# A four-layer graph network on one Trainium2 core: a column load moved to another queue, source tiles weighted on another engine, weights folded at another place

## The chip, the cores and the metric

The kernel runs on one core of a Trainium2 chip. A core has five engines that run at the same time, each with its own instruction stream, in order: TensorE (PE, matmuls), VectorE (DVE), ScalarE (ACT), GpSimd (POOL) and SyncE (SP, which here only starts DMAs). A DMA can be started from SP, ACT or POOL, and it stands in that engine's stream like any other instruction. Work areas are SBUF (125 or 128 partitions are used here) and PSUM, where matmuls accumulate. The metric is the device time of one execution in microseconds (us).

## The reference

A graph with N = 3125 nodes, 50,000 edges and D = 256 features goes through four layers. Each layer is x + gnn(norm(x)) + mix(norm(x)), then x + ffn(norm(x)). Layers 1, 2 and 3 have graph attention in the gnn part. Cut to what matters:

```python
h = (x @ W.T).reshape(n, heads, out_ch)
alpha_src = jnp.sum(h * a_src, axis=-1)
alpha_dst = jnp.sum(h * a_dst, axis=-1)
e = jax.nn.leaky_relu(alpha_src[src] + alpha_dst[dst], NEG_SLOPE)
m = jax.ops.segment_max(e, dst, num_segments=n)
e = jnp.exp(e - m[dst])
s = jax.ops.segment_sum(e, dst, num_segments=n)
alpha = e / (s[dst] + 1e-16)
out = jax.ops.segment_sum(alpha[:, :, None] * h[src], dst, num_segments=n)
```

In layers 1 and 2 this runs twice: first with four heads (of 128 features in layer 1, 64 in layer 2), then, after the bias b1, an elu and a product with W2, with one head of 256. In layer 3 it runs once, with four heads of 64; a bias gat_b is added, and the result is added to the layer's input copy before an elu. The ffn of layer 1 is a mixture of experts with a shared dense part: every node goes through the shared part, and each node's two best private experts get a copy of its row.

## The kernel before

Nodes are cut into NT = 25 tiles of P = 125. The adjacency is kept as a dense 3125 x 3125 matrix of edge counts in DRAM (`adj`).

**Edge sums.** `gat_products` does the attention for all edges by matmuls. An edge's exponential is split into factors of the source and of the target, so that exp(leaky_relu(..)) becomes max(target row, source factor) times a source weight `gpre` (L1180). First, all 25 source tiles of h, with one column of ones per head, are multiplied by `gpre` in place (L1187 to L1189): every third tile on GpSimd, the others on VectorE. Then the target tiles are taken in groups of five (875 or 750 target columns at a time in `sums_by_feature`, which is used for heads of 64). For each group the target factors are spread over all partitions (`spread`, a matmul with the identity at L189, evicted by VectorE at L78 or ScalarE at L80 into `rows`). Within a group the loop goes over the 25 source tiles s: a piece `a` of the adjacency is loaded by SP, VectorE makes t = max(rows, over) * a for each head (L1232, or L1308), and TensorE adds t and h of the tile into the accumulators `acc` (L1237, or L1313 and L1322). `gat_products` is called five times: layer 1 heads, layer 1 last, layer 2 heads, layer 2 last, layer 3.

**Last weights.** `gat_heads` loads W2 into the tile `w2a` (L1402), its bias b1, and folds the vectors a_src2 and a_dst2 into two more columns of `w2a` (`folded`, L973 multiplies, L974 reduces). It is called after the layer's input is normed, projected and mixed. Then `gat_spans` (from L1128) and the edge sums follow.

**Layer 3's local branch.** `l3_local` adds gat_b to the whole tile `local` (125 x 6400) in one GpSimd addition (L2037), and each finished target tile to its part of `local` on VectorE (L2042). `local` is loaded from DRAM in front of it, by ScalarE's queue, in two parts of 112 and 13 partitions (`halves`, L886 and L887).

**Layer 1's columns.** In layer 1's ffn each node's row with four more numbers (D + 4 columns) is scattered by GpSimd into two rows of a buffer `f1_rows` in DRAM (L2272, 50 scatters of 125 rows). The four last columns of all 8000 rows are then loaded back into `ends` (125 x 64 x 4), again by `halves` on ScalarE's queue; VectorE makes indices of it (L1585 to L1594). The shared dense part follows in program text: hidden layers with a Gelu on ScalarE (L605), products `ps_out` on TensorE, additions to X on VectorE (L1604).

**The order.** The program is traced by a tile scheduler. It places the instructions of each engine in an order of its own, with semaphores where tiles depend on each other, and it moves instructions past others of the program text. Pools of tiles reuse memory: a load into a tile waits until whoever used the place before has finished. Within an engine the order is then fixed. In the built program the additions of layer 0's last X (L931) and the first norms XN (L153) of layer 1 follow each other on VectorE; in layer 2 the XN of the first tiles stand among the last additions of X (L1653).

Of the kernel before, what the change touches and what calls it, by code (L numbers as in the profile page):

```python
# [11 lines left out]
F32 = mybir.dt.float32  # L12
# [9 lines left out]
D = 256  # L22
E = 50000
P = 125
NT = N // P
# [35 lines left out]
class Net:  # L61
# [1106 lines left out]
    def gat_products(self, far, h, al, heads, width, loops, use):  # L1168
# [3 lines left out]
        with ExitStack() as es:  # L1172
# [14 lines left out]
            for s in range(NT):  # L1187
                eng = nc.gpsimd if s % 3 == 2 else nc.vector
                eng.tensor_mul(h[:, s], h[:, s], pre[:, s, :, None].to_broadcast([P, heads, width + 1]))  # L1189
            if width < 96:  # L1190
                self.sums_by_feature(es, mine, over, h, heads, width, loops, use)
                return
# [20 lines left out]
            for g in range(NG):  # L1213
# [10 lines left out]
                for s in range(NT):  # L1224
                    a = ap.tile([P, GW], F32, name="a")
                    self.load_edges(a, self.adj_rows(), s, g)
                    if loops and s // GB == g:
                        blk = a[:, (s % GB) * P:(s % GB + 1) * P]
                        nc.vector.tensor_add(blk, blk, self.ident[:P, :P])
                    t = tp.tile([P, heads, GW], F32, name="t")  # L1230
# [21 lines left out]
    def sums_by_feature(self, es, mine, over, h, heads, width, loops, use):  # L1252
# [35 lines left out]
        for i0, n in COLUMNS:  # L1288
# [10 lines left out]
            for s in range(NT):  # L1299
                a = ap.tile([P, most], F32, name="a")  # L1300
                self.halves(nc.sync, a[:, :w], self.adj_rows()[s * P:(s + 1) * P, i0 * P:i0 * P + w])
                if loops and i0 <= s < i0 + n:
                    blk = a[:, (s - i0) * P:(s - i0 + 1) * P]
                    nc.vector.tensor_add(blk, blk, self.ident[:P, :P])
                t = []
# [86 lines left out]
    def gat_heads(self, prefix, h, al, h2, al2, heads, width, loops, eps):  # L1392
# [4 lines left out]
        h2v = h2[:, :, 0, :D]  # L1397
        with ExitStack() as es:
            wp = es.enter_context(self.pool("tg_w"))
            kp = es.enter_context(self.pool("tg_k", 2))  # L1400
            w2 = wp.tile([128, chunks, D + 2], F32, name="w2a")
            nc.sync.dma_start(w2[:, :, :D], self.ins[prefix + "W2"].rearrange("(c p) m -> p c m", p=128))  # L1402
            b1 = self.rows(wp, prefix + "b1")
            with self.pool("tg_f") as fp:
                self.folded(fp, w2[:, :, :D], chunks, 1, [prefix + "a_src2", prefix + "a_dst2"],
                            w2[:, :, D:])
# [125 lines left out]
    def l1_ffn(self, given):  # L1532
# [8 lines left out]
        with ExitStack() as es:  # L1541
# [10 lines left out]
            with ExitStack() as es2:  # L1552
# [27 lines left out]
                self.halves(nc.scalar, ends, rows[:, D:].rearrange("(q p) c -> p q c", p=P))  # L1580
# [154 lines left out]
    def layer1(self):  # L1735
# [4 lines left out]
        with self.pool("g1_h2") as low:  # L1740
            last = self.last_terms(low)
            with self.pool("g1_h") as hp:
                with self.pool("in1") as ip:
# [3 lines left out]
                self.gat_heads(pre, h, al, *last, 4, 128, False, 1e-16)  # L1747
# [189 lines left out]
    def layer2(self):  # L1937
        pre = "L2_gnn_"
        with self.pool("g2_h2") as low:
            last = self.last_terms(low)  # L1940
            with self.pool("g2_h") as hp:
                with self.pool("in2") as ip:
# [3 lines left out]
                self.gat_heads(pre, h, al, *last, 4, 64, True, 0.0)  # L1946
# [766 lines left out]
```

## Time and profile before

| What | Value |
|---|---|
| Median of 3 runs | 6647.1 us (6640.66 to 6662.06) |
| Profiled execution, its own time | 6652.58 us |
| Its span in the trace | 6650.5 us |
| Granted TensorE clock, mean | 0.911 |
| Edge sums, layer 1: heads, last | 1655 to 2304 us, 2328 to 2680 us |
| Layer 1, scatters of rows, load of `ends` | 2695 to 2769 us, 2772 to 2779 us |
| Edge sums, layer 2: heads, last | 3628 to 4150 us, 4155 to 4460 us |
| Edge sums, layer 3 | 5510 to 6048 us |

The profile names an instruction by its engine, its source line (L189 is line 189 of the kernel before), its operation, the tile that it writes and those that it reads. In a row of the timeline the first number is the start in us from the begin of the span, the second the length of the row, at its end stands the number of instructions joined in it, and in brackets the idle time of that engine before it, with what ended the idle time. A name ending in q (ACTq, SPq) is the DMA-issuing part of that engine's stream.

### The profile page before, as it was taken

To read this page: it belongs to the slowest core of one execution; us is meant where nothing else is said; L and a number is where in the kernel's file an instruction comes from. 1 tells how busy PE (TensorE), PEld (TensorE's weight loads), DVE (VectorE), ACT (ScalarE), POOL (GpSimd) and SP (SyncE) were. 2 spreads that over 40 slices of the span, in tenths; PEclk is the share of its full clock that TensorE was granted. 3 is DMA by queue.
4 is the path that set the end of the run, shared out by engine and by line. 5 is a ranking of instruction groups with operands and counts; after the bars stand their busy time and mean duration, and the time that the engine had idled before them with its cause. 6 is when DMAs were issued, how large, how long until landed. Compare 5 with 4: busy or idle time off the path is not lost. (4 is left out here: it accounts for less than half of the span.)

```text
span 6650.5 us, 80016 instructions
## 1 busy us (share of the span) xinstructions
PE 5730.2 (86%) x30063; PEld 3902.5 (59%) x30063; DVE 3734.0 (56%) x7804; ACT 1695.3 (25%) x3532; POOL 917.8 (14%) x714
## 2 busy tenths in 40 slices
PE   5887999996999998699976999999878887997876
PEld 4555975664899877468853344776534443333644
DVE  7734333128877644115036887546378888886433
ACT  2433432331011100113333011002256560003411
POOL 0000100004000012301111000120334552002021
PEclk7888999997999999789987999999889998998888
DMA  2644668101222143215520222430332223222132
GB/s 80 106 64 67 181 197 244 31 5 68 62 63 63 45 140 111 66 51 168 173 88 20 83 81 61 138 112 1 88 46 57 57 50 94 71 77 69 46 120 94
DMA packets 436886, 571.69 MB, mean 86 GB/s; under 512 B 130447, under 2 KB 321372, under 8 KB 432687
## 3 DMA queue, kind: packets, MB, share of 16 engines
q1 hardware_dynamic: 363116, 468.81, 26.4%
q10 hardware_dynamic: 44907, 68.00, 3.7%
q0 software_dynamic: 28416, 29.15, 1.6%
q8 instruction: 252, 4.13, 0.3%
q14 instruction: 195, 1.59, 0.1%
HBM read 450.03 MB, written 115.55 MB: 85 GB/s over the span
## 5 line engine op out<-in xcount | busy, mean ns | idle before, releaser
L1232 DVE SCALAR_TENSOR_TENSOR t<-rows,over,a 125x625 f32<-125x625 f32 x750 | 619.6, 866 | 426.3 <-PE acc L1237 418.9
L1308 DVE SCALAR_TENSOR_TENSOR t<-rows,over,a 125x750 f32<-125x750 f32 (+1 forms) x800 | 793.3, 1045 | 75.4 <-PE acc L1322 70.6
L1313 PE MATMUL acc<-t,g_h 125*64 125x375 f32 (+1 forms) x3200 | 596.5, 500 | 12.2 <-DVE t L1308 12.2
L1237 PE MATMUL acc<-g_h,t 125*125 125x129 f32 x5000 | 574.5, 274 | 6.2 <-ACT x L1363 3.5
L1237 PE MATMUL acc<-h,t 125*125 125x257 f32 x2500 | 558.4, 383 | 19.8 <-DVE t L1232 10.0
L1237 PEld LDWEIGHTS acc<-g_h,t 125*125 125x125 f32 x5000 | 566.2, 188 | 10.8 <-ACT x L1363 4.2
L1237 PEld LDWEIGHTS acc<-h,t 125*125 125x125 f32 x2500 | 467.3, 189 | 103.9 <-PE acc L1237 18.8
L1313 PEld LDWEIGHTS acc<-t,g_h 125*64 125x64 f32 x3200 | 220.0, 136 | 340.1 <-issue 238.8
L1322 PE MATMUL acc<-t,g_h 125*32 125x375 f32 (+1 forms) x3200 | 359.1, 496 | 0.0
L2215 POOL TENSOR_TENSOR bx<-h,crow 128x500 f32<-128x500 f32 (+1 forms) x224 | 263.7, 1195 | 308.9 <-issue 79.3
L2221 PE MATMUL y<-bx,ident 128*128 128x500 f32 (+1 forms) x448 | 222.7, 611 | 66.0 <-POOL bx L2215 64.3
L931 DVE SCALAR_TENSOR_TENSOR X<-ps_out,prob,X 125x256 f32<-125x256 f32 x200 | 87.9, 479 | 338.7 <-PE ps_out L181 338.5
L2212 DVE TENSOR_TENSOR_SCAN h<-da,state,bx 128x500 f32<-128x500 f32 (+1 forms) x224 | 246.2, 1130 | 18.3 <-ACT da L2210 15.8
L605 ACT ACTIVATE h<-ps_hidden,L_ffn_b,bn_s 128x500 f32<-128x500 f32 (+1 forms) x224 | 160.4, 723 | 350.9 <-PE ps_hidden L181 330.1
L1322 PEld LDWEIGHTS acc<-t,g_h 125*32 125x32 f32 x3200 | 99.6, 109 | 236.3 <-issue 235.5
L181 PE MATMUL ps_hidden<-xbt,w 128*128 128x250 f32 x928 | 206.2, 380 | 22.3 <-ACT xbt L166 21.9
L864 PE MATMUL agg<-h,few 125*125 125x257 bf16 x1875 | 212.6, 274 | 4.3 <-ACT few L861 2.2
L864 PEld LDWEIGHTS <-few 125*125 125x125 bf16 x1875 | 207.9, 137 | 6.1 <-ACT few L861 3.3
L181 PE MATMUL ps_out<-w,hb 128*125 128x256 f32 x928 | 205.0, 379 | 0.0
L181 PEld LDWEIGHTS ps_hidden<-xbt,w 128*128 128x128 f32 x928 | 175.1, 191 | 49.0 <-ACT xbt L166 28.6
L181 PE MATMUL ps_hidden<-XNT,L_ffn_W 128*128 128x500 f32 (+1 forms) x448 | 195.8, 562 | 0.0
L181 PEld LDWEIGHTS ps_out<-w,hb 128*125 128x125 f32 x928 | 174.0, 188 | 25.9
(765 smaller groups left out, 9461.0 us busy)
## 6 DMA issues: line engine op xcount, KB each, us to landing
a<-adj SPq DMA_DIRECT2D x500, 273.4 KB
a<-adj SPq DMA_DIRECT2D x150, 328.1 KB
arow<-adj SPq DMA_DIRECT2D x25, 1367.2 KB
adj<-block SPq DMA_DIRECT2D x22, 1531.2 KB
w<-in_L_ffn_W1p SPq DMA_DIRECT2D x29, 1024.0 KB
w<-in_L_ffn_W2p SPq DMA_DIRECT2D x29, 1024.0 KB
crow<-crows ACTq DMA_DIRECT2D x96, 250.0 KB
a<-adj SPq DMA_DIRECT2D x50, 382.8 KB
```

What stands on the lines that cost most here:

```text
L181: self.nc.tensor.matmul(ps, lhsT[k], rhs[k], start=(k == 0), stop=(k == n - 1))
L605: self.nc.scalar.activation(out[:, f, :], ps[:, :nt], func, **kw)
L864: nc.tensor.matmul(acc[b][:P, :D + 1], few[:, b * P:(b + 1) * P], h[k][:, s, :], start=(s == 0 and k == 0), stop=(s == NT - 1 and k == 2))
L931: nc.vector.scalar_tensor_tensor(x, ps, prob[:, g + j, e:e + 1], x, op0=ALU.mult, op1=ALU.add)
L1232: nc.vector.scalar_tensor_tensor(t[:, hd, :], rows[:, hd, :], over[:, s, hd:hd + 1], a, op0=ALU.max, op1=ALU.mult)
L1237: nc.tensor.matmul(acc(b, hd), t[:, hd, b * P:(b + 1) * P], h[:, s, hd, :], start=(s == 0 and first), stop=(s == NT - 1), skip_group_check ...
L1308: nc.vector.scalar_tensor_tensor(t[hd][:, :w], rows[hd][:, :w], over[:, s, hd:hd + 1], a[:, :w], op0=ALU.max, op1=ALU.mult)
L1313: nc.tensor.matmul(acc[k][c][q * width:(q + 1) * width, :c1 - c0], h[:, s, 2 * k + q, :width], t[2 * k + q][:, c0:c1], start=(s == 0), sto ...
L1322: nc.tensor.matmul(acc[pairs][c][hd * 32:(hd + 1) * 32, :c1 - c0], h[:, s1, hd, width:].to_broadcast([P, 32]), t1[hd][:, c0:c1], start=(s1 ...
L2212: nc.vector.tensor_tensor_scan(h[:, :w], da[:, :w], bx[:, :w], state[:, c, s:s + 1], op0=ALU.mult, op1=ALU.add)
L2215: nc.gpsimd.tensor_mul(bx[:, :w], h[:, :w], crow[:, :w])
L2221: nc.tensor.matmul(acc[c][:, :w], self.ident, terms[c][:, :w], start=(s == 0), stop=(s == S - 1))
```

## The change

Four edits, independent of each other in the text:

1. The weighting of the source tiles leaves the head of `gat_products`. A function `weigh(s)` does it on ScalarE, one activation with a scale per head, and is called in the loop over source tiles while the first group is worked on. This applies to all five calls.
2. The load of W2 and b1 and the fold move from `gat_heads` into `last_weights`, which is called before `layer_input` in layers 1 and 2. Their tiles live in the pool of h instead of a pool of `gat_heads`.
3. In layer 3, `local` is loaded by GpSimd's queue, and gat_b is added per target tile by VectorE in `use`, to the finished sums, instead of to all of `local` by GpSimd.
4. In layer 1's ffn, `ends` is loaded by GpSimd's queue.

```diff
@@ -1184,11 +1184,13 @@
             nc.vector.tensor_tensor(mine, mine, far[:, None, heads:].to_broadcast([P, NT, heads]), op=ALU.min)
             nc.vector.tensor_add(mine, mine, most)
             nc.scalar.activation(mine, mine, AF.Exp, scale=-0.8)
-            for s in range(NT):
-                eng = nc.gpsimd if s % 3 == 2 else nc.vector
-                eng.tensor_mul(h[:, s], h[:, s], pre[:, s, :, None].to_broadcast([P, heads, width + 1]))
+
+            def weigh(s):
+
+                for hd in range(heads):
+                    nc.scalar.activation(h[:, s, hd, :], h[:, s, hd, :], AF.Copy, scale=pre[:, s, hd:hd + 1])
             if width < 96:
-                self.sums_by_feature(es, mine, over, h, heads, width, loops, use)
+                self.sums_by_feature(es, mine, over, h, weigh, heads, width, loops, use)
                 return
             lp = es.enter_context(self.pool("gq_p", 2))
             ap = es.enter_context(self.pool("gq_a", 4))
@@ -1227,6 +1229,8 @@
                     if loops and s // GB == g:
                         blk = a[:, (s % GB) * P:(s % GB + 1) * P]
                         nc.vector.tensor_add(blk, blk, self.ident[:P, :P])
+                    if g == 0:
+                        weigh(s)
                     t = tp.tile([P, heads, GW], F32, name="t")
                     for hd in range(heads):
                         nc.vector.scalar_tensor_tensor(t[:, hd, :], rows[:, hd, :], over[:, s, hd:hd + 1], a,
@@ -1249,7 +1253,7 @@
             while jobs:
                 advance()
 
-    def sums_by_feature(self, es, mine, over, h, heads, width, loops, use):
+    def sums_by_feature(self, es, mine, over, h, weigh, heads, width, loops, use):
 
 
 
@@ -1302,6 +1306,8 @@
                 if loops and i0 <= s < i0 + n:
                     blk = a[:, (s - i0) * P:(s - i0 + 1) * P]
                     nc.vector.tensor_add(blk, blk, self.ident[:P, :P])
+                if i0 == 0:
+                    weigh(s)
                 t = []
                 for hd in range(heads):
                     t.append(tp.tile([P, most], F32, name="t"))
@@ -1389,21 +1395,25 @@
         yield
         nc.vector.scalar_tensor_tensor(x, x, 0.0, m, op0=ALU.max, op1=ALU.add)
 
-    def gat_heads(self, prefix, h, al, h2, al2, heads, width, loops, eps):
+    def last_weights(self, pool, prefix, wide):
+
+        chunks = wide // 128
+        w2 = pool.tile([128, chunks, D + 2], F32, name="w2a")
+        self.nc.sync.dma_start(w2[:, :, :D], self.ins[prefix + "W2"].rearrange("(c p) m -> p c m", p=128))
+        b1 = self.rows(pool, prefix + "b1")
+        with self.pool("tg_f") as fp:
+            self.folded(fp, w2[:, :, :D], chunks, 1, [prefix + "a_src2", prefix + "a_dst2"], w2[:, :, D:])
+        return w2, b1
+
+    def gat_heads(self, weights, h, al, h2, al2, heads, width, loops, eps):
 
         nc = self.nc
         wide = heads * width
         chunks = wide // 128
         h2v = h2[:, :, 0, :D]
+        w2, b1 = weights
         with ExitStack() as es:
-            wp = es.enter_context(self.pool("tg_w"))
             kp = es.enter_context(self.pool("tg_k", 2))
-            w2 = wp.tile([128, chunks, D + 2], F32, name="w2a")
-            nc.sync.dma_start(w2[:, :, :D], self.ins[prefix + "W2"].rearrange("(c p) m -> p c m", p=128))
-            b1 = self.rows(wp, prefix + "b1")
-            with self.pool("tg_f") as fp:
-                self.folded(fp, w2[:, :, :D], chunks, 1, [prefix + "a_src2", prefix + "a_dst2"],
-                            w2[:, :, D:])
             nc.gpsimd.memset(h2[:, :, :, D:D + 1], 1.0)
 
             def use1(pp, i, acc, eps):
@@ -1577,7 +1587,7 @@
                             for i in range(NT) for k in range(2)], "all pairs' rows differ")
 
                 ends = ep.tile([P, 2 * MAXB, 4], F32, name="ends")
-                self.halves(nc.scalar, ends, rows[:, D:].rearrange("(q p) c -> p q c", p=P))
+                self.halves(nc.gpsimd, ends, rows[:, D:].rearrange("(q p) c -> p q c", p=P))
                 who, first, w0, w1_ = (ends[:, :, k].rearrange("p (b j) -> p b j", j=2) for k in range(4))
                 e = number[:, :, None].to_broadcast([P, MAXB, 2])
                 two = [t.rearrange("p (b j) -> p b j", j=2) for t in (part, own)]
@@ -1740,11 +1750,12 @@
         with self.pool("g1_h2") as low:
             last = self.last_terms(low)
             with self.pool("g1_h") as hp:
+                weights = self.last_weights(hp, pre, 512)
                 with self.pool("in1") as ip:
                     xn, xnt = self.layer_input(ip)
                     h, al = self.l1_mix(xn, xnt, lambda: self.gat_project(
                         hp, xnt, pre, "W1", 4, ("a_src1", "a_dst1"), "g1"))
-                self.gat_heads(pre, h, al, *last, 4, 128, False, 1e-16)
+                self.gat_heads(weights, h, al, *last, 4, 128, False, 1e-16)
             self.l1_ffn(lambda xn, xnt: self.gat_last(pre, *last, False, 1e-16, xn, xnt))
 
 
@@ -1939,11 +1950,12 @@
         with self.pool("g2_h2") as low:
             last = self.last_terms(low)
             with self.pool("g2_h") as hp:
+                weights = self.last_weights(hp, pre, 256)
                 with self.pool("in2") as ip:
                     xn, xnt = self.layer_input(ip)
                     h, al = self.l2_mix(xn, xnt, lambda: self.gat_project(
                         hp, xnt, pre, "W1", 4, ("a_src1", "a_dst1"), "g2"))
-                self.gat_heads(pre, h, al, *last, 4, 64, True, 0.0)
+                self.gat_heads(weights, h, al, *last, 4, 64, True, 0.0)
             self.l2_ffn(lambda xn, xnt: self.gat_last(pre, *last, True, 0.0, xn, xnt))
 
 
@@ -2034,11 +2046,10 @@
             nc.vector.tensor_scalar(less, less, LN_EPS16, 87.0, op0=ALU.add, op1=ALU.min)
             nc.scalar.activation(less, less, AF.Exp)
 
-            nc.gpsimd.tensor_add(out, out, gb[:, None, :].to_broadcast([P, NT, D]))
-
             def use(pp, i, acc, eps):
                 x = kp.tile([P, D], F32, name="agg")
                 self.shares(kp, x, acc, 4, 64, less[:, i, :] if eps is None else eps)
+                nc.vector.tensor_add(x, x, gb)
                 nc.vector.tensor_add(out[:, i, :], out[:, i, :], x)
                 yield from self.elu(kp, out[:, i, :], "elu")
             near = nc.values_load(flag[0:1, 0:1], min_val=0, max_val=1)
@@ -2316,7 +2327,7 @@
                 wide = h.rearrange("p i h c -> p i (h c)")
                 with self.pool("g3_h") as hp:
                     local = hp.tile([P, NT, D], F32, name="local")
-                    self.halves(nc.scalar, local, rows.rearrange(by_tile, p=P))
+                    self.halves(nc.gpsimd, local, rows.rearrange(by_tile, p=P))
                     self.l3_local(local, h, al, *found)
                     lp = over.enter_context(self.pool("out_ps", 3, PSUM))
                     self.l3_join(rows, local, self.order, ys, wide, xnt, lp)
```

## The prediction

> **What bounds the kernel.** I read the busy shares first, then the timeline at each place that the diff touches, because the shares are a mean over stages with different limits.
>
> ```profile
> PE 5730.2 (86%) x30063; PEld 3902.5 (59%) x30063; DVE 3734.0 (56%) x7804; ACT 1695.3 (25%) x3532; POOL 917.8 (14%) x714
> ```
>
> TensorE is the bound for most of the span, so an edit pays only where it shortens a hole in TensorE's row, and costs only where it makes one. Each part of this change sits in such a hole. The sums are made against the profiled execution's 6652.6 us; the median of the runs is 5.5 us lower, and I subtract the same changes from it.
>
> **Weighting of the source tiles (five calls of the edge sums).** Timeline of VectorE and TensorE at the first call:
>
> ```profile
> 1657.58 17.19 DVE L1189 TENSOR_TENSOR g_h<-g_h,gpre 125x516 f32<-125x516 f32 x17 [0.79 <-ACT gpre L1180]
> 1674.70 0.41 DVE L78 COPY rows<-ps_spread 125x250 f32<-125x250 f32 x1
> ...
> 1675.16 0.99 PE L189 MATMUL ps_spread<-ident,mine 125*125 125x125 f32 x3 [14.94 <-DVE rows L78]
> 1676.13 1.22 PE L1237 MATMUL acc<-g_h,t 125*125 125x129 f32 x4
> ```
>
> TensorE idles 14.94 us for one eviction of VectorE that stands behind 17 multiplications. They go; the eviction can start when its product is there (1659.44 + 0.78 = 1660.2 instead of 1674.70): 14.5 us. At the second call the 17 multiplications of 125x257 take 8.72 us and TensorE idles some 6.2 us, at the third 9.25 and some 6.2, at the fourth 8.72 and 6.25: what goes is the idle time, not the multiplications.
>
> The work returns on ScalarE: 4 operations per source tile with four heads, 1 with one. The nearest row is the scaled copy of 125x128 of L1363, 0.36 us, so 1.4 us per tile against TensorE's 16 to 20 matmuls per tile (20 x 0.22 = 4.4 us at L1237); with one head 0.42 us (125x256, L1759) against 2.2. ScalarE is almost empty in the first group (1.42 us busy of 90), which hides it. ScalarE's own order puts its four evictions for the next group between weightings; in the two one-head calls one weighting stands behind them, and I charge 1 us each. [...] Sum: 14.5 + 5.2 + 6.2 + 5.2 = **-31 us** (bounds -38 to -24: full multiplications gone, or a quarter of it returned as waits for the first weightings).
>
> **Layer 3's local branch.** Timeline:
>
> ```profile
> 5510.70 10.18 ACTq L887 DMA_DIRECT2D local<-xn  x1
> 5520.94 0.29 ACT L2035 ACTIVATE less<-less 125x100 f32<-125x100 f32 x1 [14.70 <-DMA a<-adj]
> ...
> 5522.19 5.86 DVE L1189 TENSOR_TENSOR g_h<-g_h,gpre 125x260 f32<-125x260 f32 x17 [9.87 <-ACT gpre L1180]
> ...
> 5534.40 13.67 POOL L2037 TENSOR_TENSOR local<-local,L_gnn_gat_b 125x6400 f32<-125x6400 f32 x1 [30.70 <-SPq L2709]
> ...
> 5549.05 3.24 PE L1313 MATMUL acc<-t,g_h 125*64 125x500 f32 x6 [11.13 <-DVE t L1308]
> ```
>
> ScalarE is held 10.2 us by the issue of its own load; three exponentials stand behind it and everything else behind them. That goes with the load (-9.5). VectorE's multiplications before the first eviction go (-4). And while GpSimd adds the bias to 125x6400, one t of VectorE (normally 1.1 us) lasts 14.1 us and TensorE idles 11.13 us; 13.67 us of GpSimd inside 14.08 of VectorE: one of them shut the other out. The bias becomes 25 VectorE additions of 125x256 (0.42 us, the row of L2042), beside TensorE-bound work: -11. Together 24.5, less about 2.5 for the tiles of edge counts, which still share the DMA rings with 3.2 MB: **-22 us** (bounds -26 and -12).
>
> **Last weights folded ahead of the layer's input.** In layer 1 the fold now stands alone on the path:
>
> ```profile
> 1640.42 0.38 SPq L1402 DMA_DIRECT2D w2a<-in_L_gnn_W  x1
> ...
> 1645.69 0.76 DVE L973 TENSOR_TENSOR fold_t<-w2a,fold_a 128x256 f32<-128x256 f32 x2 [5.27 <-DMA fold_a<-in_L_gnn_a_src]
> ...
> 1651.11 0.33 DVE L1128 TENSOR_REDUCE ext<-g_al 125x4 f32<-125x100 f32 x1
> ```
>
> Load 5.27, fold 5.42: 10.7 us gone from there. But it does not become free. In the order of the built program the 16 fold operations stand between the last X addition of layer 0 and the first XN of layer 1, and the load of w2a waits for that same last addition (its memory is reused). That place in the trace:
>
> ```profile
> 1497.54 0.48 DVE L931 SCALAR_TENSOR_TENSOR X<-ps_out,prob,X 125x256 f32<-125x256 f32 x1 [2.56 <-PE ps_out L181]
> 1497.94 3.27 DVE L153 TENSOR_SCALAR XN<-X,li_mv,li_rs 125x256 f32<-125x256 f32 x6
> ```
>
> VectorE runs on without a gap and is the bound up to 1531. After: load issued 1498.0, landing some 3.5 us later (in the DMA rates of 1638 to 1652 its 512 KB are through 3.2 us after the issue), then 5.4 of fold: 8.9 us paid of the 10.7 saved, net -1.8. In layer 2 the fold was almost covered (0.5 to gain), and the new place costs more: VectorE's XN, which stood among the last X additions from 3428.09, now all wait for the last addition (about 3436), the load (3) and 8 operations (2.7), so XN starts near 3442. TensorE ran from 3434.06 to 3467 on it without holes; it starts about 11 us later and wins back perhaps 2: +9. Sum: **+7 us** (bounds -3, if the waits are covered, and +14).
>
> **Layer 1's columns on GpSimd's queue.** Timeline around the load of `ends`, 8000 elements of 16 bytes:
>
> ```profile
> 2772.18 3.71 ACTq L887 DMA_DIRECT2D ends<-f_rows  x1
> 2775.94 1.25 ACT L605 ACTIVATE hs<-ps_hidden,L_ffn_b1s 128x500 f32<-128x500 f32 x2 [54.35 <-issue]
> 2776.67 13.34 PE L181 MATMUL ps_out<-w,hs 128*125 128x256 f32 x52 [49.86 <-ACT hs L605]
> 2778.63 0.27 DVE L1585 TENSOR_TENSOR other<-ends,number 125x64 f32<-125x64 f32 x1 [67.03 <-DMA ends<-f_rows]
> ```
>
> ScalarE, waiting to issue, holds TensorE for 49.86 us. Off ScalarE's queue, TensorE does those 52 matmuls (13.3 us) and some five chunks of the next hidden layer (4) inside the hole, then is out of PSUM, because VectorE still waits for `ends` in its order ahead of the additions of X. So about 17 us of work is taken out of the time behind 2777, and the load's arrival moves by G, the time that GpSimd takes to issue 8000 elements, beside 0 now: the effect is G - 17. The trace has no plain GpSimd load. Bounds: ScalarE's queue took 0.35 + 3.71 = 4.1 us (effect -13). The indirect rows of GpSimd: 1.189 us for 125 rows against 0.894 for 16 is 2.7 ns a row; 1.295 for 125 (L2268) against the same 0.894 is 3.7; 125 against 114 rows is 6.6 (1.189 and 1.116); the whole operation per row is 9.5. G is 22, 30, 53 or 76. [...]
>
> **Sum.** -31 - 22 + 7 + 9 = -37: 6615.6 for a profiled execution, 6610 against the median.
>
> **Rivals.**
> - *GpSimd issues small elements as fast as the hardware queue.* Effect -14: 6587. [...] Against: its indirect rows grow with the number of rows.
> - *Issue at 6.6 to 9.5 ns an element.* +36 to +59: 6637 to 6660, the gain given back to the queue.
> - *Slower than before.* One place, layer 1's `ends`: if each element costs GpSimd as much as a scattered row with its pause, 1.49/125 = 11.9 ns, G = 95, +78: 6647 - 46 + 78 = 6679. With -46 from the other parts, it takes away the whole gain from G = 63 us (7.9 ns an element) and makes a measurable loss from 83 us (10.4 ns). For it: the scatters that precede it keep that pace for 74 us. Against: they fetch indices, this doesn't.
> - *The local branch doesn't gain.* If GpSimd's load crowds out the edge tiles, the second tile of edges comes as late as now (issues at 5531): -12 instead of -22, 6620.
>
> **How the numbers follow.** Chances: forecast 0.44, fast queue 0.20, 6.6 to 9.5 ns 0.20, slower 0.11, local branch 0.05. Less than 0.3% (20 us) cannot be told from no change. The first two and the last give a gain of over 20 us nearly always (0.64); the third is mostly within (0.23 with the margins of the others); slower by over 20 is the fourth with a margin, 0.13. Range 6576 to 6656: the fast queue with the upper bounds of the first two parts below, the slow slopes above.
>
> **What would show it.** Right: no multiplications between gpre and the first eviction, TensorE starting the first call within 5 us of gpre; no t over 2 us near 5535; a hole of about 9 us in VectorE before layer 1's first XN, half of it waiting for w2a; TensorE in layer 2 some 9 us late; in layer 1's dense stage a hole of TensorE that ends about 26 us later than 2777, after 52 matmuls done early. Wrong: a GpSimd issue of `ends` under 10 us or over 50, or first weightings that TensorE waits for at each tile.

## The result and the profile after

| What | Before | After |
|---|---|---|
| Median | 6645.0 us (4 runs, 6640.66 to 6662.06) | 6588.9 us (4 runs, 6584.84 to 6604.11) |
| Ratio after / before | | 0.9915 (95% interval 0.9891 to 0.9939) |
| Span of the profiled execution | 6650.5 us | 6586.6 us |
| Granted TensorE clock, mean | 0.911 | 0.915 |

The kernel became 0.85% faster, 56 us by the medians, where 37 us were forecast. The first part of the page of after, busy time by engine:

```profile
PE 5723.9 (87%) x30063; PEld 3898.5 (59%) x30063; DVE 3678.3 (56%) x7744; ACT 1791.0 (27%) x3882; POOL 863.8 (13%) x677
```

TensorE has the same 30063 matmuls, and its busy time is only 6 us shorter, so most of the 64 us of the span are holes that closed. The weighting shows as 96 us more of ScalarE. VectorE lost 56 us: 50 of multiplications and 15 in the rows of t in sums by heads of 64 (one of them was stretched before) went away, and 10 came with the 25 additions.

Where the holes were is read by landmarks, the same instruction in both traces, and the distance from one to the next. Here and below, layer 3's sums end with the start of the last row of matmuls; their true end is 1.4 us later in every run.

| From, to | Before, us | After, us | Difference |
|---|---|---|---|
| Last X addition of layer 0, first accumulation of layer 1 heads | 178.6 | 161.4 | -17.2 |
| To the last dense addition of X in layer 1's ffn | 1229.9 | 1214.3 | -15.6 |
| To the end of the last addition of the fetched rows (yg) | 531.0 | 533.0 | +2.1 |
| To the first accumulation of layer 2 heads | 207.3 | 195.4 | -11.9 |
| To layer 3's last operands (`less`) | 1864.8 | 1849.2 | -15.6 |
| To the end of layer 3's sums | 537.4 | 536.1 | -1.3 |

**Weighting.** Timeline of the first call after (start, length, then the row):

```profile
1651.91 0.97 ACT L1191 ACTIVATE g_h<-g_h,gpre 125x129 f32<-125x129 f32 x3
...
1654.32 0.42 DVE L78 COPY rows<-ps_spread 125x250 f32<-125x250 f32 x1 [3.38 <-PE ps_spread L189]
...
1655.86 1.22 PE L1241 MATMUL acc<-g_h,t 125*125 125x129 f32 x4
```

The 17.19 us of multiplications in front of L78 are gone. From `ext` (1645.87) to the first accumulation it is 10.0 us, before 25.0. A tile's weighting is four activations of 0.35 us (with one head, one of 0.50), and TensorE's only wait for an L1191 in the whole trace that the list of waits shows is one of 3.6 us.

**Layer 1's columns.** Timeline around the load:

```profile
2747.05 2.54 POOL L886 DMA_DIRECT2D ends<-f_rows  x1 [3.57 <-DMA f_rows<-XN,put]
2749.59 0.84 POOL L887 DMA_DIRECT2D ends<-f_rows  x1
2756.44 0.27 DVE L1595 TENSOR_TENSOR other<-ends,number 125x64 f32<-125x64 f32 x1 [70.25 <-DMA ends<-f_rows]
...
2759.32 8.29 PE L181 MATMUL ps_hidden<-XNT,w 128*128 128x500 f32 x12 [38.31 <-DVE X L1614]
```

GpSimd issues the 8000 elements in 2.54 + 0.84 = 3.4 us. They land 9.4 us after the start of the issue (2756.44 - 2747.05), before 6.8. TensorE's hole is 38.3 us instead of 49.9. What follows it is the next hidden layer: the 52 products `ps_out`, which stood behind the hole before, are now done ahead of it.

**Weights ahead of the input.** Timeline of VectorE at the start of layer 1, and of VectorE and TensorE at the start of layer 2:

```profile
1494.41 0.48 DVE L931 SCALAR_TENSOR_TENSOR X<-ps_out,prob,X 125x256 f32<-125x256 f32 x1 [2.56 <-PE ps_out L181]
1499.20 0.76 DVE L973 TENSOR_TENSOR fold_t<-w2a,fold_a 128x256 f32<-128x256 f32 x2 [4.31 <-DMA w2a<-in_L_gnn_W]
...
1504.62 1.71 DVE L153 TENSOR_SCALAR XN<-X,li_mv,li_rs 125x256 f32<-125x256 f32 x5
```

```profile
3405.98 0.76 DVE L973 TENSOR_TENSOR fold_t<-w2a,fold_a 128x256 f32<-128x256 f32 x2 [2.78 <-DMA w2a<-in_L_gnn_W]
...
3408.76 2.67 DVE L153 TENSOR_SCALAR XN<-X,li_mv,li_rs 125x256 f32<-125x256 f32 x8
...
3409.38 3.58 PE L164 MATMUL ps_turn<-ident,XN 125*128 125x125 f32 x16 [45.23 <-DVE XN L153]
3412.74 1.60 PE L181 MATMUL ps_h<-L_gnn_W,XNT 128*125 128x256 f32 x4
```

The price is as foreseen: 4.3 us of waiting and 5.4 of fold in layer 1; in layer 2 TensorE begins its projection 9.5 us behind the end of the last addition (3403.21), where before it began 2.9 us ahead of it.

**Layer 3.** Timeline after, at the local branch:

```profile
5448.20 1.50 POOL L886 DMA_DIRECT2D local<-xn  x1 [5.38 <-DVE less L2042]
5449.69 0.71 POOL L887 DMA_DIRECT2D local<-xn  x1
...
5463.32 1.13 DVE L1314 SCALAR_TENSOR_TENSOR t<-rows,over,a 125x875 f32<-125x875 f32 x1 [8.64 <-DMA a<-adj]
...
5464.50 1.93 PE L1319 MATMUL acc<-t,g_h 125*64 125x500 f32 x2 [7.31 <-DVE t L1314]
```

ScalarE is free at once and VectorE's first eviction is done at 5454.7, but then VectorE stands 8.64 us for the first tile of edge counts `a`. The first accumulation comes 16.6 us behind `less`, before 22.5. No t of VectorE is stretched to 14 us any more, so another 11 us should be saved right behind it; yet the whole edge sum is only 1.3 us shorter. VectorE's waits within it, before and after (engine, line, waited for: us in total, times, longest):

```profile
DVE local L1390 <- ACT elu L1388: 0.5, 1, 0.5
```

```profile
DVE local L1396 <- ACT elu L1394: 24.3, 2, 12.1
...
DVE t L1314 <- DMA a<-adj: 8.6, 1, 8.6
```

A wait that nearly didn't exist, for an exponential of the elu, has become 24.3 us. The timeline shows what is in front of it:

```profile
5674.68 0.47 ACT L80 COPY rows<-ps_spread 125x375 f32<-125x375 f32 x1 [25.00 <-PE ps_spread L189]
5675.05 0.42 ACT L1393 ACTIVATE elu<-elu 125x256 f32<-125x256 f32 x1
...
5675.95 0.42 DVE L1396 SCALAR_TENSOR_TENSOR local<-local,elu 125x256 f32<-125x256 f32 x1 [12.14 <-ACT elu L1394]
```

The elu's input was ready at 5659.9. Its exponential stands in ScalarE's stream behind an eviction of the next group's rows (L80), which waits for a product that TensorE does only 15 us later, and VectorE's next t stands behind the elu. In the built program ScalarE's order at the end of a group is changed: behind the first of these evictions stand the exponentials of two tiles, before of one.

This looks like the cost, but TensorE, which bounds the sums, does not stand still for it. Its timeline across the 12.14 us of VectorE, and then its groups of instructions in the whole edge sum (busy us, mean ns of one, idle us before; the 7.3 us lie ahead of the first accumulation):

```profile
5662.84 1.49 PE L1319 MATMUL acc<-t,g_h 125*64 125x375 f32 x8
5664.26 1.45 PE L1328 MATMUL acc<-t,g_h 125*32 125x375 f32 x6
5665.64 1.49 PE L1319 MATMUL acc<-t,g_h 125*64 125x375 f32 x8
5667.06 1.46 PE L1328 MATMUL acc<-t,g_h 125*32 125x375 f32 x10
...
5674.57 1.49 PE L1319 MATMUL acc<-t,g_h 125*64 125x375 f32 x8
```

```profile
L1319 PE MATMUL acc<-t,g_h 125*64 125x375 f32 (+1 forms) x1600 | 305.6, 502 | 7.3 <-DVE t L1314 7.3
L1328 PE MATMUL acc<-t,g_h 125*32 125x375 f32 (+1 forms) x1600 | 211.7, 497 | 0.0
L189 PE MATMUL ps_spread<-ident,mine 125*125 125x125 f32 x82 | 14.8, 309 | 0.4 <-ACT rows L80 0.4
```

Within the sums TensorE is idle for 0.4 us in all. What grew is its own work. The 1600 matmuls of the softmax denominators (L1328; a band of 32 rows of the accumulator for each head) take 211.7 us, and took 195.2 before:

```profile
L1322 PE MATMUL acc<-t,g_h 125*32 125x375 f32 (+1 forms) x1600 | 195.2, 497 | 0.0
```

The theory that the runs were to test was still the first reading: the gain comes from the weighting, the columns and a little from the weights; layer 3's edit gives nothing, because the transfer of `local` delays the edge tiles and the one step more between sums and elu changed the order on ScalarE. The rivals were that VectorE's 25 additions themselves are paid, and that part of the gain is the clock. What the runs show is that the order is the cost, but TensorE's own order and not ScalarE's; the run without gat_b has the rows for it.

### The profile page after: what moved, and what is told of

It reads as the page before. It is cut to its first block, busy times and chain, and to the rows that moved or that the text cites. A ratio compares the mean times of both kernels' runs of the same rounds, so it can differ in the third digit from the quotient of the medians.

```text
span 6586.6 us, 80498 instructions
## 1 busy us (share of the span) xinstructions
PE 5723.9 (87%) x30063; PEld 3898.5 (59%) x30063; DVE 3678.3 (56%) x7744; ACT 1791.0 (27%) x3882; POOL 863.8 (13%) x677
## 5 line engine op out<-in xcount | busy, mean ns | idle before, releaser
L1314 DVE SCALAR_TENSOR_TENSOR t<-rows,over,a 125x750 f32<-125x750 f32 (+1 forms) x800 | 778.2, 1025 | 76.3 <-PE acc L1328 64.0
L1241 PEld LDWEIGHTS acc<-g_h,t 125*125 125x125 f32 x5000 | 565.3, 188 | 11.1 <-ACT x L1369 4.4
L1328 PE MATMUL acc<-t,g_h 125*32 125x375 f32 (+1 forms) x3200 | 374.0, 496 | 0.0
L2223 DVE TENSOR_TENSOR_SCAN h<-da,state,bx 128x500 f32<-128x500 f32 (+1 forms) x224 | 246.2, 1130 | 14.1 <-ACT da L2221 10.7
L1328 PEld LDWEIGHTS acc<-t,g_h 125*32 125x32 f32 x3200 | 104.1, 109 | 246.1 <-issue 245.2
L181 PE MATMUL ps_hidden<-XNT,L_ffn_W 128*128 128x500 f32 (+1 forms) x448 | 197.8, 566 | 0.0
```

Source lines behind the costliest of these rows:

```text
L181: self.nc.tensor.matmul(ps, lhsT[k], rhs[k], start=(k == 0), stop=(k == n - 1))
L1241: nc.tensor.matmul(acc(b, hd), t[:, hd, b * P:(b + 1) * P], h[:, s, hd, :], start=(s == 0 and first), stop=(s == NT - 1), skip_group_check ...
L1314: nc.vector.scalar_tensor_tensor(t[hd][:, :w], rows[hd][:, :w], over[:, s, hd:hd + 1], a[:, :w], op0=ALU.max, op1=ALU.mult)
L1328: nc.tensor.matmul(acc[pairs][c][hd * 32:(hd + 1) * 32, :c1 - c0], h[:, s1, hd, width:].to_broadcast([P, 32]), t1[hd][:, c0:c1], start=(s1 ...
L2223: nc.vector.tensor_tensor_scan(h[:, :w], da[:, :w], bx[:, :w], state[:, c, s:s + 1], op0=ALU.mult, op1=ALU.add)
```

## The experiments

Times are medians, before in the same sessions 6647.2, 6648.3 and 6653.0 us. Up to layer 0's last addition all kernels do the same, and the ten profiled executions and the two of before and after reach it between 1494.4 and 1507.5 us. So one profile can't tell 10 us by its span; distances between landmarks of one stage repeat within 1 or 2 us in most stages (layer 1 to `ext`: 151.2 to 151.6 in the seven kernels with the same code there) and carry the readings. From layer 2's first accumulation to `less` they don't: 1849.2 to 1859.2 us in the ten kernels with the same code there.

**Columns back on ScalarE's queue.**

```diff
-self.halves(nc.gpsimd, ends, rows[:, D:]...)
+self.halves(nc.scalar, ends, rows[:, D:]...)
```

> The changed kernel with one edit undone: layer 1's columns (ends) go back to ScalarE's queue. Theory (GpSimd issues the 8000 elements in 3.4 us, and off ScalarE's queue TensorE works ahead into its hole): about 10 us slower than the changed kernel, some 6599, with TensorE out of work for about 50 us until the load has been issued instead of 38. Rival (TensorE runs out of PSUM anyway, so the queue doesn't matter): the same time within 3 us. Rival (the new queue's later landing, 9.4 us instead of 6.8, costs more than the work done ahead): up to 3 us faster.

6604.2 us, ratio to before 0.9933 (0.992 to 0.9947). TensorE's timeline:

```profile
2759.97 13.67 PE L181 MATMUL ps_out<-w,hs 128*125 128x256 f32 x52 [49.50 <-ACT hs L605]
```

The hole of 49.5 us with the 52 products behind it is back. From layer 1's first accumulation to the last dense addition it takes 1224.3 us against 1214.3: the columns on GpSimd gained 10.0 us, though they land 2.6 us later than here. Seven other kernels with the code of after at this place take 1212.3 to 1218.6 us for the stretch, so the gain is known to within some 6 to 12 us. The medians are 15 us apart; the other 5 lie within the spread between kernels.

**Local branch as before.** `local` by ScalarE's queue, gat_b by one GpSimd addition over 125x6400, the weighting left on ScalarE.

> The changed kernel with layer 3's edit undone: local by ScalarE's queue and the bias in one GpSimd addition over 125x6400; the weighting stays on ScalarE. Theory (what the first accumulation wins is eaten later in the same edge sums by 25 more VectorE additions and by eight waits of VectorE for an elu): -5 to +5 us against the changed kernel, 6584 to 6594. Rival, the sum on record (18 of its 22 us come from the queue and the bias): 18 us slower, 6607.

6586.6 us: nothing lost by undoing the edit. Rows of ScalarE's queue, VectorE, GpSimd and TensorE at the place:

```profile
5456.13 9.71 ACTq L887 DMA_DIRECT2D local<-xn  x1
...
5469.21 0.55 DVE L78 COPY rows<-ps_spread 125x375 f32<-125x375 f32 x1 [11.27 <-PE ps_spread L189]
5469.85 1.13 DVE L1314 SCALAR_TENSOR_TENSOR t<-rows,over,a 125x875 f32<-125x875 f32 x1
...
5478.84 13.86 POOL L2049 TENSOR_TENSOR local<-local,L_gnn_gat_b 125x6400 f32<-125x6400 f32 x1 [29.54 <-SPq L2721]
```

```profile
5493.69 4.22 PE L1319 MATMUL acc<-t,g_h 125*64 125x500 f32 x8 [11.34 <-DVE t L1314]
```

ScalarE's issue (9.7 us) and the hole of 11.34 us are both back, and still the stage from `less` to the end of the sums takes 530.7 us, 5.4 less than after. The first accumulation comes 17.0 us behind `less`, against 16.6. The two have different limits of about equal length. Here ScalarE's issue holds the exponential of `less`, and with it the products and evictions behind it, and the edge tile is no limit: the first t follows the eviction without waiting for `a`, which has landed 11.1 us behind `less`. In the kernel after nothing holds the evictions, but `a` has landed only 15.4 us behind `less` (11.5 in the kernel before). On GpSimd's queue the load of `local` is issued within 2.2 us, on ScalarE's it takes over 10, and beside the faster issue the small edge tile comes later.

**Weights folded late, in the pool of h.** `last_weights` is called in the argument of `gat_heads`.

```diff
-weights = self.last_weights(hp, pre, 512)
 with self.pool("in1") as ip:
...
-self.gat_heads(weights, h, al, ...)
+self.gat_heads(self.last_weights(hp, pre, 512), h, al, ...)
```

> The changed kernel with the load of W2 and the fold back in gat_heads, behind the mixing, in layers 1 and 2. Theory (layer 1 gains 2 us by the early fold, layer 2 nothing and loses nothing, because TensorE wins its late start back before the queries are done): 0 to 3 us slower, 6589 to 6592. Rival, the sum on record (the early fold costs 7 us net): 7 us faster, 6582, with layer 2's first XN and everything behind it early.

6581.8 us, ratio 0.9898 (0.9883 to 0.9913). The number fell where the recorded sum put it, but not for its reason. VectorE's timeline:

```profile
1491.45 1.38 DVE L153 TENSOR_SCALAR XN<-X,li_mv,li_rs 125x256 f32<-125x256 f32 x4
1496.53 0.88 DVE L931 SCALAR_TENSOR_TENSOR X<-ps_out,prob,X 125x256 f32<-125x256 f32 x2 [3.69 <-PE ps_out L181]
...
1501.26 0.48 DVE L931 SCALAR_TENSOR_TENSOR X<-ps_out,prob,X 125x256 f32<-125x256 f32 x1 [0.37 <-PE ps_out L181]
```

Norms XN of layer 1 now run between the last additions of layer 0, while VectorE waits for TensorE anyway. Neither the kernel before nor the one after does that. From the last addition to layer 1's first accumulation it takes 145.0 us, against 161.4 after and 178.6 before, although the fold (5.4 us) is on the path again. In layer 2 the late fold costs 2.4 us (197.8 against 195.4). Over all runs that is just outside the spread: six kernels with the early fold take 194.7 to 197.7 us here, four with the late fold 197.8 to 198.8.

**Weights exactly as before**, in `gat_heads` and in a pool of its own, to separate the place in memory from the place in time.

> The changed kernel with the load of W2 and the fold exactly as before the change: in gat_heads, in a pool of its own that reuses the input's memory. The run with the fold late but its tiles in the pool of h was 16 us faster than the changed kernel at layer 1's first accumulation. Theory (those 16 us come from where the tiles lie: the norms XN no longer wait for layer 0's last additions): here they are gone, XN starts behind the last addition, the first accumulation comes about 163 us behind it (161 in the changed kernel, 145 in that run), and the time is 0 to 4 us above the changed kernel's, some 6591. Rival (they come from folding late): first accumulation at 145 to 150, time about 6575 to 6582.

6598.3 us. VectorE's timeline:

```profile
1505.28 0.48 DVE L931 SCALAR_TENSOR_TENSOR X<-ps_out,prob,X 125x256 f32<-125x256 f32 x1 [2.56 <-PE ps_out L181]
1505.68 3.27 DVE L153 TENSOR_SCALAR XN<-X,li_mv,li_rs 125x256 f32<-125x256 f32 x6
```

XN is behind the last addition again, and the first accumulation comes 164.2 us behind it. Folding late alone does not give the 16 us, and the pool of h alone does not either (161.4 after): only the two together do, here and in the two kernels built on that run further below (145.4 and 145.6). That the pool decides which memory the input's tiles take over, and with it how early the scheduler may place XN, is my reading of it; no run shows it. Against this run the change's early fold gains 2.7 us in layer 1 and 2.4 in layer 2, the latter with the reserve just named.

**Weighting ahead of the groups again**, on VectorE and GpSimd, in all five calls.

> The changed kernel with the 25 multiplications ahead of the groups again, on VectorE and GpSimd, in all five calls. Theory (each call then waits for its first eviction behind 17 multiplications): 15 + 3.5 + 10 + 7 us in layers 1 and 2 and about 4 in layer 3, together about 39 us slower, 6628. Rival (part of the gain at these places came from the other edits or from the clock): 20 us slower or less, 6609.

6640.3 us, ratio 0.9986 (0.9977 to 0.9995). VectorE's timeline:

```profile
1658.45 17.20 DVE L1190 TENSOR_TENSOR g_h<-g_h,gpre 125x516 f32<-125x516 f32 x17 [0.74 <-ACT gpre L1180]
```

From `ext` to the first accumulation it takes 24.5 us instead of 10.0 in layer 1 heads, 15.0 instead of 11.6 in layer 1 last, and 16.3 instead of 9.2 in layer 2 last. In layer 2 heads it is 205.3 instead of 195.4 from the rows' last addition to the first accumulation. These are 35 us. Layer 3's sums take 536.4 against 536.1, no difference: without ScalarE's issue in front, the multiplications lie beside the wait for the edge tile (first accumulation 16.6 us behind `less` in both). From layer 0's last addition to the end of layer 3's sums it is 41.8 us together; the rest lies between layer 2's sums and `less`, where the spread named above covers it. Most of what the whole change brings goes away with this part.

**Without gat_b**, to see what layer 3's bias costs in any form. This run leaves out an addition that the layer needs; it is for the comparison only.

> The changed kernel without layer 3's bias gat_b (that addition is left out). The built order then has the elu's exponentials where the kernel before has them. From the last operands (less) to the end of layer 3's sums the changed kernel takes 536 us, the kernel with the old local branch 531 with a hole of 11 us in it. Theory (the per-tile bias is what eats the gain): about 519 us, the time 17 us below the changed kernel's, some 6572. Rival (the gain is eaten by the tiles of edge counts that share the rings with local): still 531 to 536, time unchanged.

6574.7 us; the stage takes 518.2 us, 17.9 less than after. VectorE's waits in it, TensorE's groups of instructions in the edge sum, and a piece of its timeline:

```profile
DVE t L1314 <- DMA a<-adj: 8.2, 1, 8.2
...
DVE local L1396 <- ACT elu L1394: 0.5, 1, 0.5
```

```profile
L1319 PE MATMUL acc<-t,g_h 125*64 125x375 f32 (+1 forms) x1600 | 304.3, 502 | 6.9 <-DVE t L1314 6.9
L1328 PE MATMUL acc<-t,g_h 125*32 125x375 f32 (+1 forms) x1600 | 193.9, 497 | 0.0
```

```profile
5683.27 0.82 PE L1328 MATMUL acc<-t,g_h 125*32 125x375 f32 x2
5684.02 1.49 PE L1319 MATMUL acc<-t,g_h 125*64 125x375 f32 x8
5685.44 1.46 PE L1328 MATMUL acc<-t,g_h 125*32 125x375 f32 x14
```

The wait for the elu is gone, that for the edge tile stays. From the first accumulation to the end of the sums it is 502.0 us, against 519.5 after and 513.7 with the old local branch: 11.7 us are the old addition's hole, 17.5 us the new form's cost.

Where do the 17.5 us lie? TensorE is idle for 0.4 us within the sums in both kernels, and the granted clock is 1.00 in both. But the same 1600 matmuls of the denominators take 193.9 us here and 211.7 after, 17.8 more, which is the whole difference. Followed matmul by matmul, the kernel after falls behind by at most 1 us a step over the second to the last group, and by only 0.6 us across VectorE's wait of 12.14 us. That wait is therefore not what is paid.

The rows show what is: the order of the matmuls on TensorE. For each two source tiles the sums need 16 of these matmuls. The single records show that up to four of them, for different heads, start within 0.02 us of each other, and the next such set starts some 0.33 us later. The 16 mostly come in two rows, with other matmuls in between. Rows of 2 and 14 take 0.82 + 1.46 = 2.28 us, in six sets; rows of 6 and 10, as shown for the kernel after, take 1.45 + 1.46 = 2.91 us, in eight. Both splits occur in both kernels, but there are 29 rows of six after and 13 here. Over the whole edge sum the matmuls go in 571 sets after and in 519 here, and 52 sets of 0.33 us are 17 us. The time of these matmuls in all twelve kernels goes with one thing: 193.9 to 196.2 us where sums and elu have no additional step between them, 211.7 to 213.5 where they have it. Why the scheduler answers one more VectorE instruction with this order on TensorE, no run shows.

**The same 25 additions on VectorE, but ahead of the sums.**

```diff
 def use(pp, i, acc, eps):
+    nc.vector.tensor_add(out[:, i, :], out[:, i, :], gb)
     x = kp.tile([P, D], F32, name="agg")
     self.shares(...)
-    nc.vector.tensor_add(x, x, gb)
```

> The changed kernel with the same 25 additions of gat_b on VectorE, but to local, ahead of the sums in each tile's work, so that the chain from the sums to the elu has one step less; the built order of ScalarE is that of the kernel before. Theory 1 (VectorE's 10.4 us are hidden; what cost was the order, eight waits of VectorE for an elu behind row evictions): layer 3's sums take 519 to 524 us, time 6572 to 6577. Theory 2 (the 10.4 us of VectorE themselves are paid): about 530 to 536 us, 6583 to 6589.

6597.9 us and 535.9 us for the stage: by these numbers alone theory 2. The waits say otherwise:

```profile
DVE local L2050 <- DMA local<-xn: 22.5, 1, 22.5
```

The scheduler put ten additions of `local` ahead of the first accumulation, where VectorE stands for 22.5 us until `local` has landed; the first accumulation comes 32.5 us behind `less` instead of 16.6. From there to the end it is 503.4 us, 1.4 more than without any bias, with the other 15 additions in it, all in the first group. The matmuls of the denominators take 196.2 us here, as in the old order. So with 25 additions, but none between the sums and the elu, TensorE's order is the old one: the order cost the 16 us, not the time of the additions (the expectations of this and an earlier run blame eight waits of VectorE; there are two, and they are not paid). But this form found another way to lose them.

**The 25 additions ahead of the sums on GpSimd.**

> As the run with VectorE's additions first, with the 25 additions of 125x256 on GpSimd. Theory (a GpSimd addition shuts VectorE out only for its own length, so that pieces with gaps cost less than one piece): holes of TensorE of 0 to 5 us, layer 3's sums 519 to 524 us, 6572 to 6577. Rival (GpSimd runs the 25 one behind the other as soon as local has landed, and shuts VectorE out as one piece did): a hole of 11 us near the landing, sums 530 us, 6583.

6593.1 us. First accumulation 15.8 us behind `less`, then 508.0 us: the stage takes 523.8 us, at the upper end of the theory. There is no hole of 11 us. GpSimd's timeline:

```profile
5493.06 54.17 POOL L2050 TENSOR_TENSOR local<-local,L_gnn_gat_b 125x256 f32<-125x256 f32 x25 [28.37 <-DMA local<-xn]
```

Now GpSimd is the one that is shut out: its 25 additions take 54 us, single ones 0.72 to 18.67 us, beside VectorE's unbroken row of t. Against the run without bias 6 us are still lost. They are lost in the first 86 us behind the first accumulation: from 40 to 60 us behind it VectorE, busy throughout, has 14 instructions in the 20 us, where the run without bias has 18, beside additions of GpSimd with a median of 1.55 us.

**Local by tile.** Built on the run with the weights folded late in the pool of h:

```diff
 def use(pp, i, acc, eps):
+    loc = kp.tile([P, D], F32, name="loc", bufs=4)
+    nc.gpsimd.dma_start(loc, rows[i * P:(i + 1) * P, :])
+    nc.gpsimd.tensor_add(loc, loc, gb)
     x = kp.tile([P, D], F32, name="agg")
     self.shares(...)
-    nc.vector.tensor_add(x, x, gb)
-    nc.vector.tensor_add(out[:, i, :], out[:, i, :], x)
+    nc.vector.tensor_add(out[:, i, :], loc, x)
```

> A version meant to beat both: the run with the fold late in the pool of h, and layer 3's local branch by tile: each tile's part of local (125x256) is loaded by GpSimd's queue into one of four rotating buffers and gat_b is added to it there by GpSimd, so that neither 3.2 MB stand in the rings before the first tiles of edge counts nor GpSimd shuts VectorE out at one place, and no step is added between the sums and the elu. Theory: the first accumulation of layer 3 comes some 8 us behind its last operands instead of 16, the rest of the sums takes 502 us as without the bias, together 510 instead of 535; layer 1 as in the run with the fold late: the time 25 us below that run's, some 6557. Rival (the first tile of edge counts is late for another reason than local's bytes): first accumulation at 15, together 517, some 6565.

6557.4 us, ratio to before 0.986 (0.9844 to 0.9877). GpSimd's and VectorE's timeline:

```profile
5441.70 2.23 POOL L2049 DMA_DIRECT2D loc<-xn  x4 [5.66 <-DVE less L2040]
...
5450.40 1.25 DVE L1314 SCALAR_TENSOR_TENSOR t<-rows,over,a 125x875 f32<-125x875 f32 x1 [2.94 <-DMA a<-adj]
```

With four tiles (0.5 MB) on the way instead of 3.2 MB the wait for the edge tile shrinks from 8.64 to 2.94 us. First accumulation 10.3 us behind `less`, then 501.3: 511.6 us in place of 536.1.

**The same with the columns on SP's queue.**

> As the version with local by tile, with layer 1's columns (ends) on SP's queue. Theory (on SP the columns land 6.8 us behind the issue as on ScalarE's queue, on GpSimd's 9.4): from layer 1's first accumulation to the last dense addition of X about 1211 us instead of 1213.4, the time 2 to 3 us lower. Rival (SP, waiting to issue, holds back the first experts' weights): the stage behind it, to the last addition of the fetched rows, 5 us or more above 531.

6553.6 us, ratio 0.9855 (0.9839 to 0.9872), not to be told from the run before it. The two issues on SP take 0.35 + 3.54 us, the columns land 6.8 us behind the first, as foreseen. But the stage to the last dense addition takes 1212.8 us against 1213.5, 0.6 us apart where kernels with the same code are up to 6 apart: the earlier landing gives nothing that can be seen here, against the 2 to 3 us expected.

## Why the prediction was right, and where not

The time, 6588.9 us, lies in the range, and the sign is right. The sum got there by errors of opposite sign: the columns came out 19 us better and the last weights 12 better than foreseen, layer 3 came out 21 worse. That so much cancelled is luck, and so is the near match with the number of the rival with the fast queue, 6587. By the prediction's own signs of being wrong, one came true: a GpSimd issue of `ends` under 10 us.

| Step | Predicted | Measured | By |
|---|---|---|---|
| Weighting | -31 | -35 | undone: 14.5, 3.4, 9.9, 7.1 |
| Layer 3's local branch | -22 | -1.3 for the stage; +5 for the edit | stage before and after; undone: 5.4 us faster |
| Last weights | +7 | -5 | exactly as before: 2.7 and 2.4 slower |
| Columns on GpSimd | +9 | -10 | undone: 10.0 slower |
| Sum | -37 | -56 by the medians | |

- **Weighting.** The mechanism and the cover hold: TensorE waited for the first eviction (from `ext` to the first accumulation 25.0 us before, 10.0 after), and ScalarE's activations (0.35 us, estimated 0.36) lie beside the first group's matmuls. Handing the work back to VectorE and GpSimd costs 35 us at the places named, and 51 by the medians. The terms 14.5 and 5.2 of layer 1 came out at 14.5 and 3.4. In layer 2 last 5.2 became 7.1. In layer 2 heads I counted 6.2 us of TensorE's idle time, while 9.9 went: TensorE's idle time in the row that I read was not all that the multiplications held up. My reading, which no run isolates, is that the evictions and spreads behind them had also run one after another.
- **Columns on GpSimd: G was mis-sized.** The +9 of the sum is G - 17 with G = 26 us, my estimate from 3.2 ns an element, the mean of the slopes 2.7 and 3.7 ns a row. No run shows that G: the issue took 3.4 us. The rows that I took are of indirect DMAs. The plain loads of the kernel after take 0.84 us for 832 elements of 16 bytes and 2.54 for 7168, which is 0.27 ns an element, and 0.71 us for 325 rows of 1 KB and 1.50 for 2800, 0.32 ns a row: about a tenth of my value. What came true is the rival with the fast queue: effect -14 foreseen (-13 by the 4.1 us of ScalarE's queue), -10 measured. The credit of 17 us for work taken out was a little large: TensorE did the 52 products and 20 matmuls of the next hidden layer, then stood still for 38.3 us. The matmul behind that hole is released by VectorE's addition of X, which reads `ps_out`; that TensorE was out of PSUM until then, as said, is my reading of it.
- **Layer 3: two terms don't add up, and one was missing.** I had added -9.5 for ScalarE's issue and -4 for the multiplications. Only 5.9 of these 13.5 us came: the first accumulation stands 22.5 us behind `less` before, 17.0 with the multiplications gone and the issue kept, 16.6 with the issue gone and the multiplications kept, and 16.6 with both gone. In the kernel after the edge tile lands only at 15.4 us; I had charged 2.5 us for that contention. The term of -11 for GpSimd's addition is right: 11.7 us between the run with the old branch and the one without the bias. "Beside TensorE-bound work" for the 25 additions is right for their own time, as far as it was tested (503.4 us with 15 of them behind the first accumulation, 502.0 with none). What was missing is TensorE's order: one step more between the sums and the elu, and the same matmuls of the denominators take 17.8 us more. I had compared the order of instructions where the fold moved, and not here. My rival for this part named the contention, at 10 us, and so had half of it.
- **Last weights.** Layer 1 was -1.8 foreseen, -2.7 measured, with the wait (4.3) and the fold (5.4) as in the sum. In layer 2 the late start is there, and larger than said (TensorE 12 us later), but "wins back perhaps 2" failed: it wins back all of it before the first accumulation. The saved fold then remains as a gain. Which work takes up the 12 us was not isolated. "VectorE runs on without a gap" up to 1531 was not quite so: it has gaps there before the change, the longest of 1.78 us.
- The rest, about 8 us of layer 2's stage to `less` and 3 us of layer 0, is at places that the change doesn't touch and within the spread between kernels with the same code there. I call no cause for it. The rival of the clock falls away: the granted clock is the same before and after where TensorE is busy nearly throughout (0.95 in layer 1 from the first accumulation on, 0.93 from there in layer 2 to `less`, 0.99 and 1.00 in layer 3's sums). It is higher only in stages where a hole closed, such as the head of layer 2 (0.75 and 0.79).

## What to carry to other kernels

One instruction more in a chain cost more here by the order of another engine than by its own duration; compare the built order of every engine in each stage that an edit touches, and first of all that of the engine that bounds the stage. A long wait on another engine need not be the cost: here VectorE waited 24 us for the elu, and across the longer of its two waits TensorE fell behind by 0.6 us, while TensorE, without a hole, took 17.8 us more for the same matmuls. A large load that isn't needed for 100 us should not be started in front of the small ones that the next instruction waits for: load it by tile through a few rotating buffers, which also spreads the work on it (here the wait for the first edge tile fell from 8.64 to 2.94 us). And when tiles move to another pool or to another place in the program, look again at where the scheduler puts their neighbours: here place and pool together decided 16 us, more than the moved work itself.

## What the runs showed of the hardware

- A plain load on GpSimd's queue was issued in 3.4 us for 8000 elements of 16 bytes and in 2.2 us for 3125 rows of 1 KB, where ScalarE's queue took 4.1 and 10.5 us in the kernel before. It landed later, though: 9.4 us behind the start of the issue for the 8000 elements, against 6.8 on ScalarE's queue and on SP's.
- Matmuls of TensorE overlap in these records, and how many do so goes with the order in its stream. The matmuls of the denominators, each about 0.5 us long and on its own band of 32 rows of the accumulator, were started up to four at once (within 0.02 us): 16 of them took 2.28 us as rows of 2 and 14, and 2.91 us as rows of 6 and 10.
- GpSimd and VectorE held each other up in both directions. Beside one GpSimd addition of 125x6400 (13.67 us) a t of VectorE took 14.1 us instead of 1.1; of 25 GpSimd additions of 125x256 single ones took up to 18.67 us beside VectorE's row of t, while the shortest took 0.72.
